# A graph layer on one core: one group of column copies moved from GpSimd's gathers to VectorE, one unchecked load a block, gates kept in PSUM, and a one-element maximum in place of a copy

## The chip, the core and the metric

The kernel runs on one core of a Trainium2 chip (trn2). The core has TensorE (PE in the profile; PEld are its weight loads), VectorE (DVE), ScalarE (ACT), GpSimd (POOL) and SyncE (SP), each with an instruction stream of its own, and DMA engines that SyncE and GpSimd feed here. The metric is the device time of one execution in microseconds; "time" is the median of several executions.

## What is computed

One layer of message passing over 12,500 nodes with 128 features and 400,000 edges, sorted by target (`dst`), each with 32 attributes. Cut to what matters:

```
h   = maximum(layernorm(x), 0)
m   = relu(concat[h[src], h[dst], ea] @ w1 + b1) @ w2 + b2
agg = segment_sum(m, dst)
gi, gh = agg @ w_ih + b_ih, h @ w_hh + b_hh
r = sigmoid(i_r + h_r); z = sigmoid(i_z + h_z); n = tanh(i_n + r * h_n)
out = x + (1 - z) * n + z * h
```

All of it is in fp32. `h[src]` is the expensive part: a row (or column) picked by a random number for each of the 400,000 edges.

## The kernel before

**Set-up.** A head normalises all nodes, keeps h transposed in SBUF (`hT_all`, 128 features x 12,500 nodes), and writes two tables to memory: A = h @ w1's first 128 rows, and B = h @ its second 128 rows + b1. It also works out, from `dst`, the first node of every group and block; SyncE, TensorE and VectorE later load such numbers into registers.

**The loop.** The edges are 3125 tiles of 128, and the tiles are 391 groups of 8 (the first has 5). One pass of the loop (`for u in range(NU)`, 782 units) does half a group. For a group, TensorE forms in PSUM the part that comes from the targets and the attributes (line 763: a one-hot matrix and the attributes in one product). The part that comes from the sources joins it in one of four ways:

- GpSimd gathers rows of A by indirect DMAs (line 193), one for each tile, eight for a group, into one of 11 buffers `G`; VectorE adds them and takes the ReLU (line 792).
- ScalarE copies columns of `hT_all`, 4 bytes in each partition, one instruction for each edge (line 1103), into a tile `HE_act`. The column's place comes from a register; 16 registers are loaded at a time (line 1090). TensorE then multiplies the tile by w1 (line 774) and VectorE takes the ReLU (line 786).
- VectorE does the same for two edges at once (class `Pairs`): one instruction (line 1061) reads two columns as bytes and writes 16-bit numbers, first + 256 x second, into `both`. For every 256 edges (`PIECE`), `part` (line 1073) parts the two bytes of each number again and writes them to `HE_dve`: 1024 bytes in each partition. A group has 512 such pairs and 4 such partings.
- SyncE fetches single rows of A by DMA.

`SPREAD` says how many groups each of VectorE, ScalarE and SyncE takes (31, 29, 5); the loop at the top spreads them evenly over the 391 groups. GpSimd has the other 326.

**Order.** Every engine's instructions stand in the order that the Python code emits them. `run_jobs` emits ScalarE's and SyncE's share of columns and rows four times a unit, evenly. VectorE's pairs are put between its other work, by due times (`some`, `behind_long`). Gathers are not issued as soon as their buffer is free: `let_go`, called four times a unit, lets one gather after another go, each behind a named instruction, twice behind VectorE's latest (`recent`) and twice behind a copy of ScalarE's (`copied`, `mark`).

**Blocks.** The sums of 14 groups make a block of 512 nodes (29 blocks; the last three are smaller). `node(b)` does a block's update as a list of steps; each `yield n` puts n units of the loop before the next step, so the steps run among the next groups' work. In order: TensorE adds up sums and degrees (tiles "nd" and "misc", one PSUM bank each); VectorE adds what the block before left over (`carry`, lines 853 and 856); TensorE makes the reset gate in "nd"; three units later ScalarE takes its sigmoid (line 902); VectorE multiplies by "misc" (line 906), adds "nd" (line 910); ScalarE takes the tanh (line 914) and the update gate's sigmoid (line 916); VectorE does the last three operations (lines 920, 923, 926); TensorE transposes, VectorE adds x (line 933), and SyncE stores. `last_node` does the last block with steps of its own. The block's first node is read by SyncE (line 830), TensorE and VectorE (line 918), and the step from the block before by VectorE (`step_of`, line 861), each with a load whose result is checked against bounds on the chip.

Of the kernel before, what the change touches and what calls it, by code (L numbers as in the profile page):

```python
# [54 lines left out]
STEP = {"act": 4, "sp": 4}  # L55
QUEUE = 10
ROW = 4 * D
SPREAD = {"dve": 31, "act": 29, "sp": 5}
START = {"dve": 14, "act": -6, "sp": 28}
SPARE = ("HE_act", "HE_dve", "G_sp")  # L60
NR = 12672
# [6 lines left out]
def tile_gnn(ctx: ExitStack, tc: tile.TileContext, x, src, srcT, dstT, dstP, eaT, eaP, w1, b1, w2T, b2,  # L68
             wih, bih, whh, bhh, out):
    nc = tc.nc  # L70
    ctx.enter_context(tc.manual_schedule())
    const = ctx.enter_context(tc.tile_pool(name="const", bufs=1))
# [108 lines left out]
    waiting, recent, copied, credit = [], [None], [None], [0]  # L181
# [140 lines left out]

    base_f = const.tile([1, NP], F32, name="base_f")
    blk_f = const.tile([1, NB], F32, name="blk_f")
    blk_i = const.tile([1, NB], I32, name="blk_i")
    off_f = const.tile([1, NB, 16], F32, name="off_f")
    off_i = const.tile([1, NB, 16], I32, name="off_i")
    base_i = const.tile([1, NB, 16], I32, name="base_i")
    step_f = const.tile([1, NB], F32, name="step_f")
    step_i = const.tile([1, NB], I32, name="step_i")  # L330
    step_c = const.tile([1, NB], F32, name="step_c")
    dloc = const.tile([128, T], F16, name="dloc")
    lim = const.tile([128, 2, NPL], F32, name="lim")
# [26 lines left out]
    def setup(pool):  # L360
        nc.vector.tensor_copy(base_f[:, 1:], base_d)
        nc.vector.memset(base_f[:, 0:1], 0.0)
        nc.vector.tensor_scalar(base_f, base_f, float(LAST), 0.0, op0=ALU.min, op1=ALU.max)
        yield
        nc.vector.tensor_copy(at_f[64:65, 512:512 + NP], base_f)
        nc.vector.tensor_tensor(at_f[64:65, :NP], at_f[64:65, 512:512 + NP], at_f[64:65, :NP], op=ALU.is_gt)
        nc.vector.tensor_reduce(beyond, at_f[64:65, :NP], AX.X, ALU.max)
        yield
        pm = ps1.tile([128, 512], F32, name="misc")
        nc.tensor.matmul(pm[:, :NP], ones, base_f, start=True, stop=True)  # L370
        nc.vector.tensor_copy(base_b[:, :, 0], pm[:, :NP])
# [10 lines left out]
        nc.vector.tensor_copy(blk_i, blk_f)  # L382
# [20 lines left out]
        nc.vector.tensor_copy(step_i, step_c)  # L403
        nc.vector.tensor_tensor(step_f, step_f, step_c, op=ALU.not_equal)
        yield
        yield
        place(0)
# [3 lines left out]
    with tc.tile_pool(name="pp", bufs=3) as pp:  # L411
# [85 lines left out]
        for q in range(NC + 3):  # L497
            if q < NC:
                b, i0, c, e, P, n0 = chunk(q)
# [3 lines left out]
            if 1 <= q <= NC:  # L503
                b, i0, c, e, P, n0 = chunk(q - 1)
# [320 lines left out]
        worked[0] = 1  # L825


    def block_start(b):
        k0, n, w = BLOCKS[b]
        g0 = nc.sync.value_load(blk_i[0:1, b:b + 1], min_val=0, max_val=N - w)  # L830
# [19 lines left out]
    def carry(b, o, p, d):  # L850
        w, last = BLOCKS[b][2], BLOCKS[max(b - 1, 0)][2]
        m = last - LEAST[b]
        nc.vector.tensor_tensor(o[:, 0:m], p[:, 0:m], o[:, bass.ds(d, m)] if b else
                                o[:, BW:BW + m], op=ALU.add)
        if m < w:
            nc.vector.tensor_copy(o[:, m:w], p[:, m:w])
        if w < last:
            nc.vector.memset(o[:, w:last], 0.0)

    def step_of(b):  # L860
        return nc.vector.value_load(step_i[0:1, b:b + 1], min_val=LEAST[b],
                                    max_val=BLOCKS[max(b - 1, 0)][2])

    def temp(w):
        return p3.tile([128, BW], F32, name="gt", bufs=3)[:, :w]

    def node(b):
        w = BLOCKS[b][2]
# [7 lines left out]
        zero(pd)  # L876
        for i in range(len(offs)):
            degree_of(b, pd, offs, i)
        d = step_of(b)
        yield 1  # L880
        carry(b, TOT, pt, d)
        carry(b, DEG[0:1, :], pd[0:1, :], d)
        worked[0] = 2
        yield 1
        g = nc.tensor.value_load(blk_i[0:1, b:b + 1], min_val=0, max_val=N - w)
# [16 lines left out]
        nc.scalar.activation(r, pr, AF.Sigmoid)  # L902
        ph = gate("misc", 3, True, False)
        yield 1
        t = temp(w)
        nc.vector.tensor_tensor(t, r, ph, op=ALU.mult)  # L906
        pi = gate("nd", 2, False, True)
        worked[0] = 2
        yield 1
        nc.vector.tensor_tensor(t, t, pi, op=ALU.add)  # L910
        pz = gate("misc", 1, True, True)
        worked[0] = 2
        yield 2 if b < NW else 1
        nc.scalar.activation(t, t, AF.Tanh)  # L914
        z = temp(w)
        nc.scalar.activation(z, pz, AF.Sigmoid)
        yield 1
        gv = nc.vector.value_load(blk_i[0:1, b:b + 1], min_val=0, max_val=N - w)
        q = r
        nc.vector.tensor_tensor(q, hT_all[:, bass.ds(gv, w)], t, op=ALU.subtract)  # L920
        worked[0] = 2
# [19 lines left out]
    def last_node():  # L941
# [5 lines left out]
        zero(pd)  # L947
        for i in range(n):
            degree_of(b, pd, offs, i)
        d = step_of(b)  # L950
        g = nc.tensor.value_load(blk_i[0:1, b:b + 1], min_val=0, max_val=N - w)
        hT = hT_all[:, bass.ds(g, w)]
        gv = nc.vector.value_load(blk_i[0:1, b:b + 1], min_val=0, max_val=N - w)
        h = hT_all[:, bass.ds(gv, w)]
        pt = ps1.tile([128, 512], F32, name="nd")[:, :w]
        zero(pt)
# [76 lines left out]
    class Pairs:  # L1033
# [35 lines left out]
        def part(self):  # L1069
            if self.turn:  # L1070
                k, p0, both = self.turn
                self.turn = None
                recent[0] = nc.vector.tensor_copy(  # L1073
                    hand[k].bitcast(U8)[:, p0 * 4:(p0 + PIECE) * 4].rearrange(
                        "p (n c b) -> p n c b", c=2, b=4),
                    both.bitcast(U8).rearrange("p n (b c) -> p n c b", c=2)).ins

    def one_by_one(m, k):
        et = {"act": ET.Activation, "sp": ET.SP}[m]
# [377 lines left out]
```

## Time and profile before

| what | value |
|---|---|
| time, median of 3 | 4675.16 us (4668.68 to 4681.94) |
| profiled execution, its time | 4666.41 us |
| profiled execution, its span | 4664.6 us |
| TensorE's granted clock, mean | 0.716 |
| DMA | 333.37 MB, mean 71 GB/s |
| gathers by GpSimd | 2605 |
| column copies by ScalarE | 29,696 |
| pairs by VectorE, partings | 15,872, 124 |

The span runs from the first to the last instruction of the program; the time holds what lies around it as well. In the rows of a profile, "idle before" is time in which an engine did nothing ahead of an instruction, with what ended it; "issue" means that nothing the profile shows ended it. ScalarE's copies overlap each other: one is shown as 189 ns long, and the next starts before it has ended, so counts per microsecond say more than durations do. Register loads are not counted as busy.

### The profile page before, as it was taken

What the parts mean: (1) busy time and instruction counts of PE and PEld (TensorE: products, weight loads), DVE (VectorE), ACT (ScalarE), POOL (GpSimd) and SP (SyncE); (2) the same over time, 40 slices, a digit from 0 to 9 for tenths busy, and PEclk for the clock granted to TensorE, in tenths of its full rate; (3) what the DMA queues carried; (4) which work ended last, traced back from release to release, by engine and by line L of the source; (5) the groups of instructions that cost most, each with busy time, mean ns of one, the idle gap of its engine ahead of it and who ended that gap; (6) DMA issues with size and microseconds to landing.
All of it is one profiled execution on the core that took longest, in us unless ns stands there. A gap on an engine that the chain in (4) does not pass through costs nothing. (4 is left out here: it accounts for less than half of the span.)

```text
span 4664.6 us, 96852 instructions
## 1 busy us (share of the span) xinstructions
PE 2538.9 (54%) x13193; PEld 1611.8 (35%) x13193; DVE 2548.3 (55%) x18124; ACT 3272.2 (70%) x29939; POOL 2485.7 (53%) x2614
## 2 busy tenths in 40 slices
PE   2465565565456455555555565455545454655657
PEld 2353342332234233323333333333323233323434
DVE  3475564564456446645654565456546555655655
ACT  2478667767767767777777767777776777676676
POOL 5345555555555555555555555555555555555551
PEclk7786767776667767776776667677767767767767
DMA  3322323222222223232222223232322322222221
GB/s 103 105 65 60 75 71 74 69 71 70 69 72 73 71 71 73 66 78 69 72 70 68 73 71 79 60 73 69 74 69 72 81 63 72 68 73 69 72 73 35
DMA packets 195490, 333.37 MB, mean 71 GB/s; under 512 B 68809, under 2 KB 117512, under 8 KB 194841
## 3 DMA queue, kind: packets, MB, share of 16 engines
q0 software_dynamic: 83360, 170.89, 16.0%
q1 hardware_dynamic: 111337, 156.20, 12.2%
q14 instruction: 539, 4.42, 0.3%
q8 instruction: 110, 1.80, 0.2%
q10 hardware_dynamic: 144, 0.07, 0.0%
HBM read 306.65 MB, written 20.24 MB: 70 GB/s over the span
## 5 line engine op out<-in xcount | busy, mean ns | idle before, releaser
L1103 ACT COPY HE_act<-hT_all 128x4 uint8 x29696 | 3169.2, 189 | 1255.9 <-issue 1223.5
L193 POOL DMA_INDIRECT G<-A,src_i x2512 | 2396.4, 954 | 2052.2 <-ACT HE_act L1103 1329.8
L1061 DVE SCALAR_TENSOR_TENSOR both<-hT_all 128x4 uint16 x15872 | 1365.4, 154 | 649.4 <-issue 635.6
L763 PE MATMUL pre<-RW,L 128*128 128x256 f32 x3128 | 1163.5, 499 | 536.3 <-DVE L L650 295.9
L763 PEld LDWEIGHTS pre<-RW,L 128*128 128x128 f32 x3128 | 681.9, 243 | 842.2 <-issue 433.3
L814 PE MATMUL seg<-RB,OH 128*32 128x129 f32 x6250 | 607.9, 325 | 270.2 <-DVE RB L792 158.4
L814 PEld LDWEIGHTS seg<-RB,OH 128*32 128x32 f32 x6250 | 334.4, 125 | 573.1 <-issue 308.9
L892 PE MATMUL nd<-DEG,brow 34*128 34x512 f32 (+2 forms) x112 | 89.0, 886 | 761.3 <-ACT gt L902 614.2
L792 DVE CUSTOM_DVE_ANT_0 RB<-pre,G 128x1024 f32<-128x1024 f32 x315 | 383.2, 1217 | 117.5 <-issue 62.9
L906 DVE TENSOR_TENSOR gt<-gt,misc 128x512 f32<-128x512 f32 (+2 forms) x28 | 18.9, 675 | 677.8 <-ACT gt L902 545.9
L892 PEld LDWEIGHTS nd<-DEG,brow 34*128 34x128 f32 x112 | 22.4, 248 | 775.7 <-ACT gt L902 620.8
L650 DVE TENSOR_TENSOR L<-L,seg 64x1024 f32<-64x1024 int32 x191 | 230.5, 1207 | 40.4 <-issue 16.4
L774 PE MATMUL pre<-w1a,HE_act 128*128 128x128 f32 x464 | 96.0, 328 | 255.0 <-ACT HE_act L1103 230.7
L786 DVE TENSOR_SCALAR RB<-pre 128x1024 f32<-128x1024 f32 x69 | 84.2, 1221 | 213.1 <-PE pre L774 154.4
L774 PEld LDWEIGHTS pre<-w1a,HE_act 128*128 128x128 f32 x464 | 90.0, 235 | 271.2 <-ACT HE_act L1103 235.6
L703 DVE TENSOR_TENSOR OH<-dloc,seg 128x512 f32<-128x512 f16 (+1 forms) x198 | 132.9, 672 | 17.6 <-issue 17.6
L842 PE MATMUL nd<-spot,sums 128*128 128x40 f32 x782 | 139.0, 358 | 2.8 <-DVE sums L823 2.8
L842 PEld LDWEIGHTS nd<-spot,sums 128*128 128x128 f32 x782 | 134.6, 270 | 13.7 <-issue 10.6
L1073 DVE COPY HE_dve<-both 128x1024 uint8<-128x1024 uint8 x124 | 88.6, 715 | 24.8 <-issue 15.7
L774 PEld LDWEIGHTS pre<-w1a,HE_dve 128*128 128x128 f32 x496 | 90.3, 226 | 14.1 <-remote 2.0
L920 DVE TENSOR_TENSOR gt<-hT_all,gt 128x512 f32<-128x512 f32 (+2 forms) x28 | 19.1, 680 | 134.3 <-ACT gt L914 109.3
L774 PE MATMUL pre<-w1a,HE_dve 128*128 128x128 f32 x496 | 89.3, 309 | 3.0 <-remote 1.7
(185 smaller groups left out, 1473.5 us busy)
## 6 DMA issues: line engine op xcount, KB each, us to landing
G_sp<-A SPq DMA_DIRECT2D x5120, 0.5 KB
L<-in_dstP SPq DMA_DIRECT2D x195, 256.0 KB
L<-in_eaP SPq DMA_DIRECT2D x195, 256.0 KB
G<-A,src_i POOLq DMA_INDIRECT x2512
RW<-B SPq DMA_DIRECT2D x782, 16.0 KB
xb<-in_x SPq DMA_DIRECT2D x26, 256.0 KB
out<-xb SPq DMA_DIRECT2D x26, 256.0 KB
xs<-in_x SPq DMA_DIRECT2D x11, 512.0 KB
```

The lines of the kernel that those rows point to most:

```text
L193: fetched = nc.gpsimd.indirect_dma_start(out=G[k][:, j, a, :], out_offset=None, in_=x if k < RAW else A, in_offset=bass.IndirectOffsetOnAx ...
L650: recent[0] = nc.vector.tensor_tensor(o.rearrange("v (k e) -> v k e", k=m), i.rearrange("v (k e) -> v k e", k=m), SEGB[(k // 2) % 2][:2 * ...
L703: recent[0] = nc.vector.tensor_tensor(p, dloc[:, e0:e1, None].to_broadcast(shape), row[:, None, :].to_broadcast(shape), op=ALU.is_equal).ins
L763: nc.tensor.matmul(p[:, 2 * i:2 * i + 2, :], Ls[k // QP][:, c0:c0 + 128], RW[k % 4], start=True, stop=not raw)
L774: nc.tensor.matmul(p[:, 2 * i + a, :], cols, w1a, start=False, stop=n + 1 == len(l) or l[n + 1][1] != j)
L792: made = nc.vector._custom_dve(TENSOR_ADD_SAT, out=o, in0=p, in1=G[k].rearrange("p j a f -> p (j a) f")[:, c, :], s0=float("inf"), s1=0.0)
L814: nc.tensor.matmul(p[r0:r0 + V, :D + 1], OH[k][:, a * GRP + j, :], RB[k % 2][:, 2 * j + a, :D + 1], start=False, stop=all(b != a for _, _, ...
L842: nc.tensor.matmul(p[:, bass.ds(offs[i], V + SHIFT)], sums[:, slot(b, i), :D], spot[:, i % 2, :], start=False, stop=i == len(offs) - 1)
L892: nc.tensor.matmul(pg, brow[:, c], DEG[:, :w], start=True, stop=False)
L1061: recent[0] = nc.vector.scalar_tensor_tensor(self.both[:, e % PIECE // 2, :], column(second), 256.0, column(first), op0=ALU.mult, op1=ALU. ...
L1073: recent[0] = nc.vector.tensor_copy(hand[k].bitcast(U8)[:, p0 * 4:(p0 + PIECE) * 4].rearrange("p (n c b) -> p n c b", c=2, b=4), both.bitc ...
L1103: copied[0] = nc.scalar.copy(he[:, e * 4:e * 4 + 4], column(v)).ins
```

## The change

Five things are altered:

- VectorE takes 32 groups of columns in place of 31; GpSimd keeps 325. VectorE's first group is then number 20 and not 21, and the places of some of VectorE's and ScalarE's groups move by one or a few.
- The parting of pairs (`part`) is a reduction by maximum over an added axis of length one. It gives the same bytes as the copy.
- The tiles `blk_i` and `step_i` go. Their numbers stand in two free columns of `off_i`, and VectorE loads both with one load a block, without a check on the chip; SyncE's and TensorE's loads of the first node have no check either.
- The carries of the sums and of the degrees lie a unit apart (in the last three blocks they follow at once, as before).
- In `node`, the candidate gate's sum is written back to its PSUM tile, where tanh is taken in place, and the update gate's sigmoid is taken in place in PSUM as well; the product r x h goes to r's own tile.

```
--- before.py
+++ after.py
@@ -55,7 +55,7 @@
 STEP = {"act": 4, "sp": 4}
 QUEUE = 10
 ROW = 4 * D
-SPREAD = {"dve": 31, "act": 29, "sp": 5}
+SPREAD = {"dve": 32, "act": 29, "sp": 5}
 START = {"dve": 14, "act": -6, "sp": 28}
 SPARE = ("HE_act", "HE_dve", "G_sp")
 NR = 12672
@@ -322,12 +322,10 @@
 
     base_f = const.tile([1, NP], F32, name="base_f")
     blk_f = const.tile([1, NB], F32, name="blk_f")
-    blk_i = const.tile([1, NB], I32, name="blk_i")
     off_f = const.tile([1, NB, 16], F32, name="off_f")
     off_i = const.tile([1, NB, 16], I32, name="off_i")
     base_i = const.tile([1, NB, 16], I32, name="base_i")
     step_f = const.tile([1, NB], F32, name="step_f")
-    step_i = const.tile([1, NB], I32, name="step_i")
     step_c = const.tile([1, NB], F32, name="step_c")
     dloc = const.tile([128, T], F16, name="dloc")
     lim = const.tile([128, 2, NPL], F32, name="lim")
@@ -379,7 +377,6 @@
             nc.vector.tensor_scalar(blk_f[:, b0:b1_], base_f[:, k0:k0 + (b1_ - b0 - 1) * n + 1:n], float(N - w),
                                     None, op0=ALU.min)
         yield
-        nc.vector.tensor_copy(blk_i, blk_f)
         nc.vector.memset(off_f, 0.0)
         off_c = pool.tile([128, NB * 16], F32, name="off_c", bufs=1)[:1, :].rearrange("o (b n) -> o b n", n=16)
         yield
@@ -400,7 +397,8 @@
         nc.vector.tensor_copy(off_i, off_c)
         yield
         nc.vector.tensor_tensor(off_f, off_f, off_c, op=ALU.not_equal)
-        nc.vector.tensor_copy(step_i, step_c)
+        nc.vector.tensor_copy(off_i[:, :, 14], step_c)
+        nc.vector.tensor_copy(off_i[:, :, 15], blk_f)
         nc.vector.tensor_tensor(step_f, step_f, step_c, op=ALU.not_equal)
         yield
         yield
@@ -825,9 +823,15 @@
         worked[0] = 1
 
 
+    def first_of(engine, b):
+        _, (g,) = nc.values_load_multi_w_load_instructions(
+            off_i[0:1, b, 15:16], engines=[engine], min_val=0, max_val=N - BLOCKS[b][2],
+            skip_runtime_bounds_check_because="clamped above")
+        return g
+
     def block_start(b):
         k0, n, w = BLOCKS[b]
-        g0 = nc.sync.value_load(blk_i[0:1, b:b + 1], min_val=0, max_val=N - w)
+        g0 = first_of(ET.SP, b)
         xb = p3.tile([128, 4, D], F32, name="xb", bufs=2)[:w // 4, :, :]
         put(xb, x[bass.ds(g0, w), :].rearrange("(p i) f -> p i f", i=4))
         _, offs = nc.values_load_multi_w_load_instructions(
@@ -858,8 +862,11 @@
             nc.vector.memset(o[:, w:last], 0.0)
 
     def step_of(b):
-        return nc.vector.value_load(step_i[0:1, b:b + 1], min_val=LEAST[b],
-                                    max_val=BLOCKS[max(b - 1, 0)][2])
+        _, (d, g) = nc.values_load_multi_w_load_instructions(
+            off_i[0:1, b, 14:16], engines=[ET.DVE], min_val=0, max_val=N - BLOCKS[b][2],
+            skip_runtime_bounds_check_because="clamped above")
+        return nc.s_assert_within(d, LEAST[b], BLOCKS[max(b - 1, 0)][2],
+                                  skip_runtime_bounds_check_because="clamped above"), g
 
     def temp(w):
         return p3.tile([128, BW], F32, name="gt", bufs=3)[:, :w]
@@ -876,13 +883,16 @@
         zero(pd)
         for i in range(len(offs)):
             degree_of(b, pd, offs, i)
-        d = step_of(b)
+        d, gv = step_of(b)
         yield 1
         carry(b, TOT, pt, d)
+        worked[0] = 2
+        if b < NW:
+            yield 1
         carry(b, DEG[0:1, :], pd[0:1, :], d)
         worked[0] = 2
         yield 1
-        g = nc.tensor.value_load(blk_i[0:1, b:b + 1], min_val=0, max_val=N - w)
+        g = first_of(ET.PE, b)
         hT = hT_all[:, bass.ds(g, w)]
 
         def gate(name, i, with_h, with_s):
@@ -902,20 +912,18 @@
         nc.scalar.activation(r, pr, AF.Sigmoid)
         ph = gate("misc", 3, True, False)
         yield 1
-        t = temp(w)
-        nc.vector.tensor_tensor(t, r, ph, op=ALU.mult)
-        pi = gate("nd", 2, False, True)
+        nc.vector.tensor_tensor(r, r, ph, op=ALU.mult)
+        t = gate("nd", 2, False, True)
         worked[0] = 2
         yield 1
-        nc.vector.tensor_tensor(t, t, pi, op=ALU.add)
+        nc.vector.tensor_tensor(t, r, t, op=ALU.add)
         pz = gate("misc", 1, True, True)
         worked[0] = 2
         yield 2 if b < NW else 1
         nc.scalar.activation(t, t, AF.Tanh)
-        z = temp(w)
-        nc.scalar.activation(z, pz, AF.Sigmoid)
+        z = pz
+        nc.scalar.activation(z, z, AF.Sigmoid)
         yield 1
-        gv = nc.vector.value_load(blk_i[0:1, b:b + 1], min_val=0, max_val=N - w)
         q = r
         nc.vector.tensor_tensor(q, hT_all[:, bass.ds(gv, w)], t, op=ALU.subtract)
         worked[0] = 2
@@ -947,10 +955,9 @@
         zero(pd)
         for i in range(n):
             degree_of(b, pd, offs, i)
-        d = step_of(b)
-        g = nc.tensor.value_load(blk_i[0:1, b:b + 1], min_val=0, max_val=N - w)
+        d, gv = step_of(b)
+        g = first_of(ET.PE, b)
         hT = hT_all[:, bass.ds(g, w)]
-        gv = nc.vector.value_load(blk_i[0:1, b:b + 1], min_val=0, max_val=N - w)
         h = hT_all[:, bass.ds(gv, w)]
         pt = ps1.tile([128, 512], F32, name="nd")[:, :w]
         zero(pt)
@@ -1070,10 +1077,10 @@
             if self.turn:
                 k, p0, both = self.turn
                 self.turn = None
-                recent[0] = nc.vector.tensor_copy(
+                recent[0] = nc.vector.tensor_reduce(
                     hand[k].bitcast(U8)[:, p0 * 4:(p0 + PIECE) * 4].rearrange(
                         "p (n c b) -> p n c b", c=2, b=4),
-                    both.bitcast(U8).rearrange("p n (b c) -> p n c b", c=2)).ins
+                    both.bitcast(U8).rearrange("p n (b c) -> p n c b", c=2)[:, :, :, :, None], AX.X, ALU.max).ins
 
     def one_by_one(m, k):
         et = {"act": ET.Activation, "sp": ET.SP}[m]
```

More of the change, by code (lines that the diff above doesn't have):

```diff
@@ L57 @@
 ROW = 4 * D
-SPREAD = {"dve": 31, "act": 29, "sp": 5}
+SPREAD = {"dve": 32, "act": 29, "sp": 5}
 START = {"dve": 14, "act": -6, "sp": 28}
@@ L324, in tile_gnn @@
     blk_f = const.tile([1, NB], F32, name="blk_f")
-    blk_i = const.tile([1, NB], I32, name="blk_i")
     off_f = const.tile([1, NB, 16], F32, name="off_f")
@@ L329, in tile_gnn @@
     step_f = const.tile([1, NB], F32, name="step_f")
-    step_i = const.tile([1, NB], I32, name="step_i")
     step_c = const.tile([1, NB], F32, name="step_c")
@@ L381, in setup @@
         yield
-        nc.vector.tensor_copy(blk_i, blk_f)
         nc.vector.memset(off_f, 0.0)
@@ L402, in setup @@
         nc.vector.tensor_tensor(off_f, off_f, off_c, op=ALU.not_equal)
-        nc.vector.tensor_copy(step_i, step_c)
+        nc.vector.tensor_copy(off_i[:, :, 14], step_c)
+        nc.vector.tensor_copy(off_i[:, :, 15], blk_f)
         nc.vector.tensor_tensor(step_f, step_f, step_c, op=ALU.not_equal)
@@ L825, in take, with first_of @@
         worked[0] = 1
+    def first_of(engine, b):
+        _, (g,) = nc.values_load_multi_w_load_instructions(
+            off_i[0:1, b, 15:16], engines=[engine], min_val=0, max_val=N - BLOCKS[b][2],
+            skip_runtime_bounds_check_because="clamped above")
+        return g
     def block_start(b):
         k0, n, w = BLOCKS[b]
-        g0 = nc.sync.value_load(blk_i[0:1, b:b + 1], min_val=0, max_val=N - w)
+        g0 = first_of(ET.SP, b)
         xb = p3.tile([128, 4, D], F32, name="xb", bufs=2)[:w // 4, :, :]
@@ L860, in step_of @@
     def step_of(b):
-        return nc.vector.value_load(step_i[0:1, b:b + 1], min_val=LEAST[b],
-                                    max_val=BLOCKS[max(b - 1, 0)][2])
+        _, (d, g) = nc.values_load_multi_w_load_instructions(
+            off_i[0:1, b, 14:16], engines=[ET.DVE], min_val=0, max_val=N - BLOCKS[b][2],
+            skip_runtime_bounds_check_because="clamped above")
+        return nc.s_assert_within(d, LEAST[b], BLOCKS[max(b - 1, 0)][2],
+                                  skip_runtime_bounds_check_because="clamped above"), g
     def temp(w):
@@ L878, in node @@
             degree_of(b, pd, offs, i)
-        d = step_of(b)
+        d, gv = step_of(b)
         yield 1
         carry(b, TOT, pt, d)
+        worked[0] = 2
+        if b < NW:
+            yield 1
         carry(b, DEG[0:1, :], pd[0:1, :], d)
@@ L884, in node @@
         yield 1
-        g = nc.tensor.value_load(blk_i[0:1, b:b + 1], min_val=0, max_val=N - w)
+        g = first_of(ET.PE, b)
         hT = hT_all[:, bass.ds(g, w)]
@@ L904, in node @@
         yield 1
-        t = temp(w)
-        nc.vector.tensor_tensor(t, r, ph, op=ALU.mult)
-        pi = gate("nd", 2, False, True)
+        nc.vector.tensor_tensor(r, r, ph, op=ALU.mult)
+        t = gate("nd", 2, False, True)
         worked[0] = 2
         yield 1
-        nc.vector.tensor_tensor(t, t, pi, op=ALU.add)
+        nc.vector.tensor_tensor(t, r, t, op=ALU.add)
         pz = gate("misc", 1, True, True)
@@ L914, in node @@
         nc.scalar.activation(t, t, AF.Tanh)
-        z = temp(w)
-        nc.scalar.activation(z, pz, AF.Sigmoid)
+        z = pz
+        nc.scalar.activation(z, z, AF.Sigmoid)
         yield 1
-        gv = nc.vector.value_load(blk_i[0:1, b:b + 1], min_val=0, max_val=N - w)
         q = r
@@ L949, in last_node @@
             degree_of(b, pd, offs, i)
-        d = step_of(b)
-        g = nc.tensor.value_load(blk_i[0:1, b:b + 1], min_val=0, max_val=N - w)
+        d, gv = step_of(b)
+        g = first_of(ET.PE, b)
         hT = hT_all[:, bass.ds(g, w)]
-        gv = nc.vector.value_load(blk_i[0:1, b:b + 1], min_val=0, max_val=N - w)
         h = hT_all[:, bass.ds(gv, w)]
@@ L1072, in part @@
                 self.turn = None
-                recent[0] = nc.vector.tensor_copy(
+                recent[0] = nc.vector.tensor_reduce(
                     hand[k].bitcast(U8)[:, p0 * 4:(p0 + PIECE) * 4].rearrange(
                         "p (n c b) -> p n c b", c=2, b=4),
-                    both.bitcast(U8).rearrange("p n (b c) -> p n c b", c=2)).ins
+                    both.bitcast(U8).rearrange("p n (b c) -> p n c b", c=2)[:, :, :, :, None], AX.X, ALU.max).ins
     def one_by_one(m, k):
```

## The prediction

> **What bounds the kernel now.** I read the page first, then the waits of each engine, then stretches of the loop side by side. The page:
>
> ```profile
> span 4664.6 us, 96852 instructions
> ...
> PE 2538.9 (54%) x13193; PEld 1611.8 (35%) x13193; DVE 2548.3 (55%) x18124; ACT 3272.2 (70%) x29939; POOL 2485.7 (53%) x2614
> ```
>
> No engine looks full; ScalarE (ACT) is the busiest. The waits of ScalarE (engine, line, released by: us in total, times, longest) say what its other 30% is:
>
> ```profile
> ACT HE_act L1103 <- issue: 1223.5, 2104, 1.9
> ...
> ACT gt L991 <- PE pre L972: 22.1, 1, 22.1
> ...
> ACT HE_act L1103 <- ACT HE_act L1103: 0.7, 3, 0.3
> ```
>
> In the whole loop ScalarE waits for nobody. Its 1223.5 us of pauses between column copies are "issue": nothing that the profile shows holds it. The one real wait, 22.1 us, comes after the last copy. The copies fill the run:
>
> ```profile
> L1103 ACT COPY HE_act<-hT_all x29696: 176/189/198, 168.1 to 4632.6; 128x4 uint8 x200
> ```
>
> They start at 168.1 us and end at 4632.6; 32.0 us later the program is over. So time = 168.1 + the chain of 29,696 copies + 32.0. VectorE, by contrast, stands and waits, mostly for ScalarE (the rows of line 786 through TensorE's products of ScalarE's columns):
>
> ```profile
> DVE gt L906 <- ACT gt L902: 545.9, 22, 36.2
> DVE RB L786 <- PE pre L774: 154.4, 19, 25.6
> DVE gt L920 <- ACT gt L914: 109.3, 22, 7.2
> DVE gt L906 <- ACT HE_act L1103: 86.6, 4, 31.3
> ...
> DVE gt L906 <- remote: 45.3, 2, 30.3
> ```
>
> Together 941.5 us of slack on VectorE. GpSimd has slack too; in the groups (busy, mean ns | idle before, released by):
>
> ```profile
> L193 POOL DMA_INDIRECT G<-A,src_i x2512 | 2396.4, 954 | 2052.2 <-ACT HE_act L1103 1329.8 <-issue 538.8 <-DMA dst_i<-in_dstT 77.2
> L1061 DVE SCALAR_TENSOR_TENSOR both<-hT_all 128x4 uint16 x15872 | 1365.4, 154 | 649.4 <-issue 635.6
> ```
>
> The gathers are released behind ScalarE's copies and wait 1329.8 us for them. Why then does ScalarE pause? Two timelines of the same 10 us, GpSimd's and ScalarE's:
>
> ```profile
> 2011.74 0.94 POOL L193 DMA_INDIRECT G<-A,src_i  x1 [3.92 <-ACT HE_act L1103]
> ...
> 2016.73 0.95 POOL L193 DMA_INDIRECT G<-A,src_i  x1 [0.30 <-issue]
> ```
> ```profile
> 2009.09 6.10 ACT L1103 COPY HE_act<-hT_all 128x4 uint8 x60 [1.13 <-issue]
> 2016.02 0.38 ACT L1103 COPY HE_act<-hT_all 128x4 uint8 x3 [0.84 <-issue]
> 2017.45 0.38 ACT L1103 COPY HE_act<-hT_all 128x4 uint8 x3 [1.04 <-issue]
> ```
>
> Five gathers start back to back from 2011.74; from the third or fourth on, ScalarE falls from 60 copies in 6.1 us to 3 in about 1.4. It pauses when gathers come in a row. Stretches of the loop (us; then busy time and instructions of PE, PEld, DVE, ACT, POOL; granted clock, DMA share, GB/s) give the price:
>
> ```profile
> 170.00:4590.00 4420.00, 2409.57 (x12506) 1509.47 (x12507) 2429.85 (x17551) 3164.43 (x29359) 2416.20 (x2533) 0.71 0.29 71
> 4590.00:4632.00 42.00, 34.78 (x203) 23.19 (x204) 25.33 (x139) 41.01 (x409) 0.00 (x0) 0.85 0.14 40
> 2011.00:2043.00 32.00, 1.69 (x14) 1.17 (x12) 0.00 (x0) 25.52 (x246) 18.86 (x20) 0.55 0.32 76
> 2070.00:2102.00 32.00, 20.57 (x109) 12.64 (x109) 23.23 (x160) 21.26 (x197) 16.56 (x18) 0.77 0.28 74
> 1846.00:1882.00 36.00, 0.00 (x0) 0.00 (x0) 0.38 (x4) 29.33 (x278) 22.47 (x24) 0.50 0.28 67
> 1884.00:1920.00 36.00, 25.74 (x131) 15.57 (x130) 24.62 (x169) 27.43 (x252) 21.02 (x22) 0.79 0.31 74
> ```
>
> ScalarE does 6.64 instructions per us in the loop (29,359 in 4420), 9.7 once the gathers are over (409 in 42). Beside VectorE and TensorE at rest it does 7.7 (246 in 32; 278 in 36), beside both at work 6.2 and 7.0: on the mean 1.1 per us less.
>
> **The change, part by part.** ScalarE keeps its 29 groups, so only what alters the pace of its copies counts.
>
> *One group from GpSimd to VectorE.* Eight gathers go (2605 to 2597), 512 pairs come. If ScalarE's pauses belong to the gathers evenly, one costs 1223.5/2605 = 0.47 us, eight 3.8. The bounds: zero, and the whole loop per gather, 4420/2533 = 1.745 us, eight 14.0. I take -3.8, since pauses are what a gather was seen to cause. A group on VectorE costs (1365.4 + 649.4)/31 = 65 us with its register loads; that lies in the 941.5 us of slack. But VectorE at work slows ScalarE: 65 us at 1.1 per us are 72 copies, at 6.64 per us 10.8 us. In the rows compared TensorE works too, and its work does not grow: of the 378 instructions of PE, PEld and DVE in the stretch from 2070, 160 are VectorE's, 42%: 4.6 us. I take +4.6, with 0 and 10.8 as bounds.
>
> *The maximum for the copy.* No one-element maximum is in the trace. The copy:
>
> ```profile
> L1073 DVE COPY HE_dve<-both 128x1024 uint8<-128x1024 uint8 x124 | 88.6, 715 | 24.8 <-issue 15.7 <-DVE both L1061 7.2 <-remote 1.8
> ```
>
> The nearest rows are another operation over 1024 elements, and a reduction of 160 elements to one:
>
> ```profile
> L792 DVE CUSTOM_DVE_ANT_0 RB<-pre,G 128x1024 f32<-128x1024 f32 x315 | 383.2, 1217 | 117.5 <-issue 62.9 <-PE pre L763 24.2 <-DVE both L1061 22.2
> ```
> ```profile
> L357 DVE TENSOR_REDUCE lim<-dloc 128x1 f32<-128x160 f16 (+2 forms) x20 | 6.3, 316 | 0.7
> ```
>
> The copy's 715 ns for 1024 elements is far under line 792's 1217; the reduction, with 316 ns for 160, shows no such speed. At the pace of line 792 the maximum takes 1.22 us; 128 of them 156.2, against 88.6: 67.6 us more on VectorE. If a result for every element costs an element's time again, it is about 2.3 us, 294 in all, 206 more; if it kept the copy's pace, only the four more, 3 us. Nearest is line 792, for its 1024 results: 1.22. All this lies in the slack; on ScalarE's chain 0, since it adds four instructions. If being busy alone disturbed ScalarE, 67.6 us at the price above would be 11.2. The Trainium skill speaks against this edit (VectorE: DVE Perf Modes, section on the perf-mode tier table): a copy has a two-element mode, the reduction none, 1227 against 2293 ns for 2048 fp32 elements. By that ratio a part takes 1.34 us as an estimate, 83 us more in all; the slack covers this as well, so the sum stays.
>
> *One unchecked load a block.* A checked load on VectorE:
>
> ```profile
> L861 DVEq TENSOR_LOAD <-step_i x29: 304/307/619, 387.6 to 4638.2; - x29
> L861 DVEq FUSED_REGOPS  x29: 183/190/210, 388.0 to 4638.9; - x29
> L861 DVEq SEQ_ASSERT  x29: 23/23/41, 388.3 to 4639.1; - x29
> ```
>
> 0.52 us; two in each of 29 blocks, 30 us, become 29 loads without the two other steps, 9 us: -21 us on VectorE, the same steps gone from TensorE and SyncE, none on ScalarE: 0. VectorE's sum is 65 + 67.6 - 21 = +112 us, and 830 us of slack remain. Were this cover gone, the 112 us would all be on the path.
>
> *Carries apart.* The degree's carry comes one unit later and so does everything behind it in a block; a block's steps take 20 of 28 units in place of 19, so the next block isn't touched, and ScalarE meets its sigmoid one unit later among copies that it does anyway: 0.
>
> *Gates in PSUM.* Tanh and the second sigmoid write PSUM, and tanh reads it:
>
> ```profile
> L914 ACT ACTIVATE gt<-gt 128x512 f32<-128x512 f32 (+2 forms) x28 | 17.2, 615 | 0.0
> ...
> L916 ACT ACTIVATE gt<-misc 128x512 f32<-128x512 f32 (+2 forms) x28 | 15.8, 565 | 0.6 <-issue 0.6
> ```
>
> A PSUM source is 50 ns cheaper: -1.4 us for 28 tanhs. A PSUM result is not in the trace; I take no difference, 1.4 either way. The banks "nd" and "misc" are held up to the products on VectorE, but their next users come behind those products already: no new wait.
>
> Sum on ScalarE's chain: -3.8 + 4.6 - 1.4 = -0.6 us, nothing. Against the profiled execution's 4666.4 us that is 4666; the median of the runs shown, 4675.2, lies 8.8 higher, so I put the forecast at 4675. About 0.3%, 14 us, is what a measurement can tell from no change.
>
> **The rivals.** *Slower: ScalarE is disturbed by VectorE's time, not by its instructions.* All 112 us at 1.1 copies per us cost 123 copies, 18.6 us, and with the least relief from gathers (0) and none from PSUM, 4694. It decides from 0.83 copies per us on (14 us). For it: both pairs of stretches. Against it: TensorE is in both.
>
> *Slower by far: VectorE becomes the bound.* That needs a maximum of (941.5 - 65 + 21 + 88.6)/128 = 7.7 us; at 10 us the time would be near 4970. No row points to that.
>
> *Faster: the copy's hold on GpSimd goes.* Against a floor of 944 ns for a gather, the 2512 of line 193 take 25 us too long in sum (954 - 944 = 10 ns each); if the copies cause that, and the rows of gathers then start later and end later over ScalarE, up to 25 us come back: 4650. With the other bound of the eight gathers alone (-14.0) 4661. The Trainium skill (SBUF — State Buffer, section on who interferes with whom) has this rule: a copy in a two-port mode takes the port pair shared with GpSimd for the whole instruction, a reduction on trn2 never does. Against a gain: GpSimd waits 1329.8 us for ScalarE, so its own delays are not on the path.
>
> **How the numbers follow.** No change within 14 us: 0.48. Faster by the hold or the gathers: 0.26. Slower by VectorE's time: 0.23, by a very dear maximum 0.03. The range reaches to the rivals: down to 4645, which is 4650 without the 4.6 us that the forecast charges for the pairs; up to 4702, the slower rival at its worse pair of stretches (7.69 - 6.16 = 1.53 copies per us, 25.8 us) without the 1.4 of PSUM. The likeliest case's own range is 4661 to 4689.
>
> **What would show it.** Right: ScalarE's copies 29,696 with issue pauses of 1200 to 1250 us and no wait on others in the loop; the waits of lines 906, 920 and 786 on VectorE shorter by some 110 us; 128 maxima near 1.2 us; 16,384 pairs; 2597 gathers. Wrong: ScalarE waiting for VectorE or TensorE at a gate, pauses outside 1200 to 1250, or a maximum above 7 us.

## The result and the profile after

The changed kernel takes 4697.22 us against 4678.12 (medians of 6 runs each): ratio 1.0042, interval 1.0032 to 1.0052. It is slower by 19 us, more than the 14 us inside which "no change" was forecast. The profiled execution took 4693.54 us against 4666.41, 27 us more; the one of before lies 12 us under its median and the one after 4, so about 8 of the 27 are chance.

The experiments below were spread over five chips. On three of them the kernel before takes 4607 to 4677 us, on the other two 3321 and 3323; every ratio is to the kernel before on the same chip. One of the 23 executions of the kernel before on the second chip took 7719 us and is left out of its ratios.

The page after, as it was quoted of before:

```profile
span 4691.4 us, 97156 instructions
...
PE 2571.0 (55%) x13209; PEld 1630.1 (35%) x13209; DVE 2656.7 (57%) x18640; ACT 3276.2 (70%) x29939; POOL 2459.8 (52%) x2606
```

VectorE is busy 108 us longer, ScalarE as long as before. ScalarE's copies (instructions: shortest, middle, longest ns, first and last start in us) and the waits of its copies and of its last gate, from two views:

```profile
L1110 ACT COPY HE_act<-hT_all x29696: 176/189/207, 168.0 to 4659.7; 128x4 uint8 x200
```
```profile
ACT HE_act L1110 <- issue: 1244.4, 2138, 2.6
...
ACT gt L998 <- PE pre L979: 21.2, 1, 21.2
```

The frame of the prediction stands: head 168.0 us, tail 31.7, and the chain of copies between them, which sets the time. All that was lost was lost inside the chain, 27.2 us, and no new wait shows there: its pauses without a visible cause grew from 1223.5 to 1244.4. VectorE's waits for ScalarE, and the groups that the change touches:

```profile
DVE gt L915 <- ACT gt L912: 508.9, 23, 36.0
DVE RB L784 <- PE pre L772: 101.6, 18, 24.9
DVE gt L928 <- ACT nd L923: 93.4, 18, 7.7
...
DVE gt L915 <- ACT HE_act L1110: 60.6, 3, 25.8
...
DVE gt L915 <- remote: 20.9, 1, 20.9
```
```profile
L193 POOL DMA_INDIRECT G<-A,src_i x2504 | 2370.4, 947 | 2097.7 <-ACT HE_act L1110 1409.1
L1068 DVE SCALAR_TENSOR_TENSOR both<-hT_all 128x4 uint16 x16384 | 1406.5, 154 | 644.0 <-issue 629.5
...
L1080 DVE TENSOR_REDUCE HE_dve<-both 128x1024 uint8<-128x1024 uint8 x128 | 155.3, 1213 | 29.7 <-issue 19.7
```
```profile
L923 ACT ACTIVATE nd<-nd 128x512 f32<-128x512 f32 (+2 forms) x28 | 15.8, 566 | 0.6 <-issue 0.6
```

VectorE still waits 785.4 us in these five rows (the five of before gave 941.5, and some 110 less was forecast): it isn't the bound here. A maximum takes 1213 ns (1.22 us was forecast), the tanh in PSUM 566 (565 was forecast), and the mean gather has become 7 ns shorter.

The whole loop and its end without gathers, in the views that gave ScalarE's pace before (time, then busy us and instructions of PE, PEld, DVE, ACT, POOL):

```profile
170.00:4590.00 4420.00, 2424.21 (x12443) 1517.63 (x12443) 2518.86 (x17932) 3140.89 (x29092) 2390.27 (x2525) 0.70 0.29 70
4617.00:4659.00 42.00, 34.90 (x205) 23.35 (x205) 24.29 (x128) 41.53 (x413) 0.00 (x0) 0.84 0.11 33
```

ScalarE does 6.58 instructions per us beside the gathers in place of 6.64, and still 9.8 without them.

### The profile page after: what moved, and what is told of

Same layout as the page of the kernel before. It is cut to its first block, busy times and chain, and to the rows that moved or that the text cites. A ratio compares the mean times of both kernels' runs of the same rounds, so it can differ in the third digit from the quotient of the medians.

```text
span 4691.4 us, 97156 instructions
## 1 busy us (share of the span) xinstructions
PE 2571.0 (55%) x13209; PEld 1630.1 (35%) x13209; DVE 2656.7 (57%) x18640; ACT 3276.2 (70%) x29939; POOL 2459.8 (52%) x2606
## 5 line engine op out<-in xcount | busy, mean ns | idle before, releaser
L1110 ACT COPY HE_act<-hT_all 128x4 uint8 x29696 | 3173.5, 189 | 1278.4 <-issue 1244.4
L193 POOL DMA_INDIRECT G<-A,src_i x2504 | 2370.4, 947 | 2097.7 <-ACT HE_act L1110 1409.1
L1068 DVE SCALAR_TENSOR_TENSOR both<-hT_all 128x4 uint16 x16384 | 1406.5, 154 | 644.0 <-issue 629.5
L812 PE MATMUL seg<-RB,OH 128*32 128x129 f32 x6250 | 624.1, 332 | 404.1 <-DVE RB L790 241.1
L1080 DVE TENSOR_REDUCE HE_dve<-both 128x1024 uint8<-128x1024 uint8 x128 | 155.3, 1213 | 29.7 <-issue 19.7
L906 PE MATMUL nd<-TOT,w2ih 128*128 128x512 f32 (+2 forms) x112 | 91.8, 915 | 0.0
```

Of the source, the lines that this page charges most:

```text
L193: fetched = nc.gpsimd.indirect_dma_start(out=G[k][:, j, a, :], out_offset=None, in_=x if k < RAW else A, in_offset=bass.IndirectOffsetOnAx ...
L812: nc.tensor.matmul(p[r0:r0 + V, :D + 1], OH[k][:, a * GRP + j, :], RB[k % 2][:, 2 * j + a, :D + 1], start=False, stop=all(b != a for _, _, ...
L1068: recent[0] = nc.vector.scalar_tensor_tensor(self.both[:, e % PIECE // 2, :], column(second), 256.0, column(first), op0=ALU.mult, op1=ALU. ...
L1080: recent[0] = nc.vector.tensor_reduce(hand[k].bitcast(U8)[:, p0 * 4:(p0 + PIECE) * 4].rearrange("p (n c b) -> p n c b", c=2, b=4), both.bi ...
L1110: copied[0] = nc.scalar.copy(he[:, e * 4:e * 4 + 4], column(v)).ins
```

## The experiments

Each run is named by its number, e1 to e18. Theories: **A**, VectorE's 512 more pairs slow ScalarE's copies beside them. **B**, the copy's hold on GpSimd's ports kept gathers from following each other; without it rows get longer and ScalarE pauses more. **C**, VectorE's busy time in general disturbs ScalarE (the slower rival of the prediction). **D**, the edits in the blocks cost.

**One part taken back, one part alone.** Four kernels on one chip (the kernel before: 4606.8 us).

The changed kernel with the copy back (e1):

```
-                recent[0] = nc.vector.tensor_reduce(
+                recent[0] = nc.vector.tensor_copy(
...
```

> The changed kernel with the copy back in place of the maximum; all else as changed. The changed kernel stands 19 us (0.42%) over the one before. Theory A (the 512 more pairs and their loads slow ScalarE's copies beside them, as instructions): still +15 to +20 us. Theory B (the copy's hold on the port pair parted rows of gathers; without it the rows are longer and ScalarE pauses more): 0 to +5 us. Theory C (VectorE's longer busy time disturbs ScalarE, whatever it does): 0 to +7 us, by the 67 us that the copy saves of 112. Theory D (the edits in the blocks): still +19 us. Under A and D rows of five or more gathers stay as frequent as in the changed kernel (253 of 672 rows), under B they fall back to some 230 of 721.

Measured: 1.0047 (1.0033 to 1.0060). Rows of five or more gathers, counted as starts at most 1.4 us apart, are 264 of 721 in its trace, 256 of 746 in that of before and 276 of 707 after the change; they decide nothing.

The changed kernel with `"dve": 31` (e2):

> The changed kernel with 31 groups on VectorE in place of 32, the maximum and the block edits kept. A: 0 to +5 us over the kernel before. B: still +15 to +20. C: +8 to +12 (VectorE busy some 47 us more than before). D: +19.

Measured: 1.0022 (1.0009 to 1.0034).

The kernel before with the maximum alone (e3, the opposite of the first diff):

> The kernel before with the maximum in place of the copy, nothing else. A: 0. B: +15 to +20 us and longer rows of gathers. C: +11 (67 of 112 us of VectorE's time). D: 0.

Measured: 1.0013 (0.9998 to 1.0027).

The kernel before with `"dve": 32` alone (e4):

> The kernel before with 32 groups on VectorE in place of 31, nothing else. A: +15 to +20 us. B: 0 to +3. C: +8 to +11 (65 us of VectorE's time). D: 0.

Measured: 1.0015 (1.0003 to 1.0028).

B falls: with the copy back the kernel is as slow as ever. C is in trouble for the same reason, since the copy saves VectorE some 65 us. Neither A nor D explains the whole: 32 groups alone cost 7 us where A wanted 15 to 20, and the other edits with 31 groups (e2) 10 us where D wanted 19.

**The blocks alone, and the prices made large.** Four kernels on a second chip (before: 4608.43 us). The block edits alone, with 31 groups and the copy (e5):

> The kernel before with the block edits alone (one unchecked load a block, carries apart, gates in PSUM); 31 groups, the copy. The first four runs left, by sums, 0.1 to 0.3% for these edits (with the copy back the changed kernel stood at 1.0047, 32 groups alone at 1.0015; 31 groups at 1.0022, the maximum alone at 1.0013). Theory D (the block edits cost most of it): 1.002 to 1.003. Theory A (VectorE's pairs) with no cost in the blocks: 1.000.

Measured: 1.0009 (0.9997 to 1.0021), +4 us.

Half of the pairs left out (e6). Each instruction that stays writes its sum to two places, so that the columns of every second pair are missing:

```
-                recent[0] = nc.vector.scalar_tensor_tensor(
-                    self.both[:, e % PIECE // 2, :], column(second), 256.0, column(first),
...
+                if self.done % 2 == 0:
+                    at2 = e % PIECE // 2
+                    recent[0] = nc.vector.scalar_tensor_tensor(
+                        self.both[:, at2:at2 + 2, :], column(second)[:, None, :].to_broadcast([128, 2, 4]), 256.0,
...
```

> The kernel before with every second pair instruction left out: one instruction writes the same sum to two places, so half of the columns on VectorE are wrong, and 7936 instructions fewer run there; register loads, copies, gathers and their order stay. Theory A (ScalarE's pace beside VectorE's instructions: 7 us for 512 pairs and their loads, so some 14 ns a pair): 4607 less 100 to 130 us. If VectorE's instructions are off ScalarE's chain altogether: 0 to -10 us.

Measured: 4559.29 us (two runs), 0.9894 (0.9869 to 0.9919), -49 us. That is 6.2 ns for each of the 7936 pairs left out, so 3.2 us for 512 of them, less than half of what A needs, and less than the 4.6 us of the prediction. Taken as a price of VectorE's time it can be had from the pages of e5 and e6, on the same chip:

```profile
PE 2565.2 (55%) x13193; PEld 1623.8 (35%) x13193; DVE 2544.1 (55%) x18124; ACT 3272.2 (71%) x29939; POOL 2482.4 (54%) x2614
```
```profile
PE 2498.1 (55%) x13193; PEld 1592.1 (35%) x13193; DVE 1971.8 (43%) x10188; ACT 3264.7 (72%) x29939; POOL 2495.3 (55%) x2614
```

VectorE is busy 572 us less, so the price is 0.09 us for each of them, half of what C takes (1.1 copies per us at 6.64 copies per us, 0.17). At half its price C gives some 10 of the 19 us.

28 groups on ScalarE, 32 on VectorE (e7):

```
-SPREAD = {"dve": 31, "act": 29, "sp": 5}
+SPREAD = {"dve": 32, "act": 28, "sp": 5}
```

> The kernel before with 28 groups on ScalarE and 32 on VectorE: one group moves from ScalarE to VectorE, gathers stay. If the copies' chain bounds (time = head + copies + tail), with pauses that belong to the gathers: 1024 copies at 0.105 us go, -108 us, +7 for the pairs: -100 us. If pauses scale with the copies: -154 + 7 = -147. If something shared by all engines bounds, and not ScalarE's own chain: within 15 us of the kernel before.

Measured: 4554.39 us (two runs), 0.9883 (0.9858 to 0.9908), -54 us: less than any reckoning by the copies' own time, more than nothing. Its chain of copies and its pauses, and after them those of the next kernel (e8), which keeps 29 groups on ScalarE, and has 36 on VectorE and 40 gathers fewer:

```profile
L1103 ACT COPY HE_act<-hT_all x28672: 176/189/197, 168.8 to 4520.9; 128x4 uint8 x200
```
```profile
ACT HE_act L1103 <- issue: 1207.7, 2133, 1.9
```
```profile
L1103 ACT COPY HE_act<-hT_all x29696: 176/189/197, 169.0 to 4575.0; 128x4 uint8 x200
```
```profile
ACT HE_act L1103 <- issue: 1156.2, 2095, 1.9
```

With 1024 copies fewer the pauses are not fewer but 51 us more (and 21 us more than the 1186.7 of e5, which has as many gathers as e7): they don't scale with the copies. A copy costs 151.8 ns there (4352.1 us by 28,672) and 148.4 here. So ScalarE's chain is what ends last, but only half of the 108 us of which it was to be relieved is gained; the single traces put 21 to 51 us of the rest down to pauses.

36 groups on VectorE, 321 on GpSimd (e8):

> The kernel before with 36 groups on VectorE and 321 on GpSimd: five groups moved where the change moves one. If the cost is one of the pairs and linear: five times the 7 us of 32 groups, +35 us (1.0076). If 32 groups cost by their places among the other groups and not by their number: within 10 us of the kernel before. If fewer gathers relieve ScalarE by 0.47 us each with nothing against it: -19 us.

Measured: 1.0011 (0.9998 to 1.0023), +5 us for five groups, 1 us each. This speaks against C: five groups are 325 us of VectorE's time, which at C's price would cost 54 us less the relief from 40 gathers, 19 us at the prediction's 0.47 us for a gather. No run measured that relief by itself; at the prediction's upper bound of 1.745 us for a gather (70 us) it would hide C. The 1 us is also what the prediction's two terms gave for a group (-3.8 + 4.6 = +0.8). The 7 us of e4 (1 to 13) can't then be the price of a group: they are chance in part, or belong to the places of the groups.

**Which block edit, beside 32 groups.** Four kernels on a third chip (before: 4677.35 us). The changed kernel again (e9):

> The changed kernel itself, beside the three below on one chip: 1.004 to 1.005 of the kernel before, as on record (1.0042). If the single edits only add up (32 groups 0.15%, the maximum 0.13%, the blocks 0.09%): 1.0037. With the copy back it stood at 1.0047, so by that pair the maximum costs nothing, by the single edit 0.13%.

Measured: 1.0048 (1.0035 to 1.0060).

The three others have 32 groups and the copy, and one block edit each is taken back. Both carries in one step (e10):

```
         carry(b, TOT, pt, d)
-        worked[0] = 2
-        if b < NW:
-            yield 1
         carry(b, DEG[0:1, :], pd[0:1, :], d)
```

> 32 groups, the copy, unchecked loads, gates in PSUM, but both carries in one step as before. If the later carry (every step of a block a unit later) is what makes 32 groups dear with the block edits (1.0047 with all of them, 1.0015 without any): 1.0015 to 1.002. If not: 1.004 to 1.005.

Measured: 1.0013 (1.0000 to 1.0025).

The gates' tiles in SBUF (e11):

```
-        nc.vector.tensor_tensor(r, r, ph, op=ALU.mult)
-        t = gate("nd", 2, False, True)
+        t = temp(w)
+        nc.vector.tensor_tensor(t, r, ph, op=ALU.mult)
+        pi = gate("nd", 2, False, True)
...
-        z = pz
-        nc.scalar.activation(z, z, AF.Sigmoid)
+        z = temp(w)
+        nc.scalar.activation(z, pz, AF.Sigmoid)
```

> 32 groups, the copy, unchecked loads, carries apart, but the gates' tiles in SBUF as before. If holding the PSUM banks longer, or ScalarE's writes to PSUM, cost: 1.0015 to 1.002. If not: 1.004 to 1.005.

Measured: 1.0005 (0.9994 to 1.0016).

The loads checked, from `blk_i` and `step_i`, as before (e12):

> 32 groups, the copy, carries apart, gates in PSUM, but the checked loads as before. Loads off ScalarE's chain: 1.004 to 1.005. If the unchecked loads let VectorE, TensorE and SyncE run on where their sequencers stood, and that disturbs ScalarE: 1.0015 to 1.003. If the three block edits are noise and 32 groups stand at 1.0015 whatever is beside them, all three kernels lie at 1.001 to 1.003.

Measured: 1.0035 (1.0023 to 1.0048). So with 32 groups the later carry and the gates in PSUM seem to cost some 0.3% together, and either of them without the other next to nothing (theory **E**); the loads are off it. Against E stands e5, where both together, beside 31 groups, cost 0.09%. The alternative (theory **F**): the steps' and groups' places happen to fall well or badly.

**Four kernels on a chip without the pauses** (before: 3321.05 us). They were meant to part E from F and to try ScalarE's pauses. The changed kernel with the carries together (e13), and with 33 groups (e14):

> The changed kernel with both carries in one step, all else as changed. Theory E (the later carry together with the gates in PSUM costs 0.2 to 0.35%; either alone does not): 1.001 to 1.002. If the later carry matters only beside the copy: 1.004 to 1.005.

Measured: 1.0181 (1.0167 to 1.0195), +61 us.

> The changed kernel with 33 groups on VectorE in place of 32. If the cost is that of the block edits whenever VectorE has more work (E): 1.004 to 1.006. Theory F (it hangs on how the groups' places fall beside the blocks' steps, so that one more group can take it away): 1.000 to 1.003, as with 31 groups (1.0022).

Measured: 1.0371 (1.0356 to 1.0385), +124 us. A small write of GpSimd's behind every gather in the kernel before (e15):

```
             fetched = nc.gpsimd.indirect_dma_start(
...
+            nc.gpsimd.memset(idle_t, 0.0)
```

> The kernel before with a small write of GpSimd's (a tile of zeros that nothing reads) behind every gather, about 0.2 to 0.25 us, so that gathers in a row start some 1.5 us apart and not 1.25. If ScalarE pauses because gathers follow too close: fewer than 24% of the loop with four gathers in the last 5 us, and 40 to 150 us less. If it pauses for the number of gathers, not their distance: within 15 us of the kernel before, or slower, since rows take longer.

Measured: 1.0920 (1.0903 to 1.0936). 26 groups on ScalarE and 34 on VectorE (e16):

> The kernel before with 26 groups on ScalarE and 34 on VectorE (three groups moved from ScalarE to VectorE). One group gave -54 us (28 on ScalarE): three give -160, 0.966, if ScalarE's chain still bounds; with VectorE's waits for ScalarE then used up, it and not ScalarE is late, and the gain is smaller, -60 to -120.

Measured: 1.0696 (1.0680 to 1.0712).

None answers its question, since the pauses are missing there. Slowing the gathers costs there (in e15 VectorE waits 355.6 us for landings), and so does work moved to VectorE: three groups from ScalarE 231 us (e16), and the 33rd group, between e13 and e14, 62 us, where the prediction reckons 65 us for a group's work.

```profile
DVE RB L794 <- DMA G<-A,src_i: 355.6, 102, 10.0
```

**The changed kernel (e17) and its carries together (e18), once more** (a fifth chip, again without pauses, before: 3323.15 us):

> The changed kernel, beside the one with the carries together. On a chip where ScalarE pauses beside the gathers (the kernel before at 4600 to 4700 us): 1.004 to 1.005, as twice. On a chip where it does not (the kernel before at 3321 us): VectorE has no slack there, so the 112 us of its sum count; with the carries together it stood at 1.0181 (+61 us), so 1.015 to 1.035.

Measured: 1.0179 (1.0165 to 1.0193), +57 us.

> The changed kernel with both carries in one step. On a chip with pauses, theory E (the later carry with the gates in PSUM costs 0.2 to 0.35%): 1.001 to 1.002; theory F (accident of places): anything from 1.000 to 1.005. On a chip without: 1.0181 as before, and the changed kernel equal to it within 10 us if the later carry is off the path there.

Measured: 1.0184 (1.0170 to 1.0198). The later carry is nothing there. The changed kernel's page on this chip, ScalarE's copies and waits, and what is left of VectorE's idle time, most of it ahead of its own pairs:

```profile
PE 2435.7 (72%) x13209; PEld 1573.3 (47%) x13209; DVE 2619.7 (78%) x18640; ACT 3098.1 (92%) x29939; POOL 2464.5 (73%) x2606
```
```profile
L1110 ACT COPY HE_act<-hT_all x29696: 177/189/207, 93.9 to 3340.1; 128x4 uint8 x200
```
```profile
ACT nd L923 <- DVE nd L919: 83.2, 19, 8.4
ACT gt L912 <- PE nd L906: 58.9, 10, 16.1
ACT HE_act L1110 <- issue: 31.2, 78, 1.1
```
```profile
DVE both L1068 <- issue: 465.2, 790, 1.8
DVE RB L790 <- issue: 37.7, 75, 1.3
DVE RB L790 <- DVE both L1068: 30.8, 54, 0.8
DVE L L648 <- issue: 25.4, 46, 1.2
DVE RB L790 <- PE pre L761: 19.6, 29, 3.6
```

Here the picture is turned round: ScalarE's pauses are 31.2 us in place of 1244.4, and it waits 83.2 and 58.9 us at the gates for VectorE and TensorE, while no wait for ScalarE is among VectorE's long ones. VectorE's cover is gone. For that case the prediction put all of its 112 us on the path; the kernel lost 57. The kernel before has no trace on such a chip, so which of these waits are new isn't shown.

## Why the prediction was wrong

*What held.* ScalarE's chain sets the time (head and tail moved by less than half a microsecond; a group taken off ScalarE gives 54 us). A group moved from GpSimd to VectorE has a price of about 1 us (e8), as the two terms together had it. That is in part luck: a pair costs 6.2 ns (e6), so the second term was 3.2 and not 4.6, and the first was never measured by itself. The maximum takes 1213 ns, tanh and the second gate are as cheap as reckoned, no gate made ScalarE wait. The rule that the reduction leaves GpSimd's ports alone (the Trainium skill, SBUF — State Buffer, section on who interferes with whom) agrees with the mean gather's 947 ns after 954: in the traces of all chips with pauses it is 953 to 958 ns beside copies and 946 to 950 beside maxima. As the argument against that rival said, it bought nothing: GpSimd waits 1409.1 us for ScalarE. By the ratio of the other page (the Trainium skill, VectorE: DVE Perf Modes, section on the perf-mode tier table) the maximum was to take 1.34 us, an estimate; 1213 ns decides for the row of line 792.

*What failed.* The sum on ScalarE's chain, -0.6 us, by its noughts: "on ScalarE's chain 0" for the maximum, 0 for the carries apart, "no new wait" for the gates in PSUM, and by the step of pricing each edit alone and adding up. Each of the three parts alone measured a little above its term: 32 groups +7 us (1.4 to 13) for +0.8, the maximum +6 (-1 to 12) for 0, the blocks +4 (-1.4 to 10) for -1.4. Their sum, 0.37%, lies within the interval of the whole (0.32 to 0.52%). But the kernel with the copy back speaks against a plain sum: without the maximum 0.24% is left to expect, and e1 measured 0.47% (0.33 to 0.60), as much as the whole. By that the maximum's nought held, and as far as these runs tell it is the noughts of the carries and gates that failed, beside 32 groups: with the copy in all three, the loss is 0.35% where both edits are there (e12, its loads checked), 0.13% without the later carry (e10), 0.05% without the gates in PSUM (e11). Beside 31 groups the same two edits cost 0.09% (e5).

*By what.* By ScalarE's pauses for the most part: of the 27.2 us by which the traced chain is longer, 20.9 are pauses and 4.3 the copies' own busy time. These are single executions, and they vary by as much: the traced one of e5 took 23 us more than the median of its kernel. The traces of the third chip agree, with pauses of 1243 and 1244 us in e9 and e12, 1232 and 1235 in e10 and e11. The prediction had the price of pauses from two pairs of stretches, where VectorE and TensorE stood or worked, and spread it over VectorE's instructions. The slower rival took the same price for VectorE's time and came to 4694, close to the 4697 measured. That is luck as far as the runs show: by it the copy put back should have returned 11 us (returned: none), and five groups cost 54 less the relief from the gathers (cost: 5). At the half price of e6 the rival isn't excluded, but it then explains half of the loss at most.

One reading of the prediction holds on some chips only: that pauses are what a gather causes. In the trace after the change ScalarE loses 0.39 us in each us to pauses where three or more gathers have started within the last 5 us, and 0.04 where fewer have. On two chips the gathers follow each other for long stretches, and ScalarE hardly pauses. What the chips differ in isn't shown. The marks set for right or wrong were also too weak: "pauses of 1200 to 1250 us" was met at 1244.4.

*What stays open.* Which edit the loss belongs to. In e1 and e9 to e12 it seems to need 32 groups, the later carry and the gates in PSUM together; that would be an effect of how the steps fall in time. For the whole change the single edits with their intervals allow a plain sum as well; for e1 they are 0.23% short, where the three intervals together allow some 0.22%. Why ScalarE should pause more for these edits no run shows. Repeats of the changed kernel with the carries together on a chip with pauses would part the two; both runs of it fell on chips without. That the pauses depend on the distance between gathers was tried only where there are none.

*A better kernel.* None is shown to be faster on all chips. 28 groups on ScalarE and 32 on VectorE gained 1.17% where ScalarE pauses; 26 and 34 lost 7% where it doesn't, and neither was run on the other kind of chip.

## What to carry to other kernels

An engine that stands and waits is cover only as long as the engine it waits for is slow, and here that was a matter of the chip: in the changed kernel VectorE waits 785 us in the rows shown on one chip, and next to nothing for ScalarE on another. The same edits, which make a slack engine longer, cost 19 us on the one and 57 on the other, so such an edit should be priced for both. And where an engine's idle time is "issue", released by nothing that the profile shows, a term of half a percent can't be had by sums of a few us each. Prices were to be had by making an edit large (half the pairs, five groups), and even these didn't add up to the loss: edits that go in together should be measured together.

## What the runs showed of the hardware

Unexpected was the difference between chips. Of the five chips of the experiments, three ran the kernel before in 4607 to 4677 us and two in 3321 and 3323, 28 to 29% less, with hardly any spread among their runs (3319 to 3326). In the traces of the changed kernel the copies start at 93.9 us in place of 168.0; ScalarE's pauses are 31.2 us in place of 1244.4, and the chain of 29,696 copies, with what lies between them, takes 109 ns for each (3246.2 us in all) in place of 151. On the chip without pauses gathers run at the same 1.25 us apart, for ten in a row in this stretch (of which the first and the last are shown):

```profile
1999.66 0.94 POOL L193 DMA_INDIRECT G<-A,src_i  x1 [0.30 <-issue]
...
2010.90 0.98 POOL L193 DMA_INDIRECT G<-A,src_i  x1 [0.30 <-issue]
```

In e13, on the other such chip, ScalarE makes 52 copies in 5.35 us beside four gathers in a row:

```profile
1999.83 5.35 ACT L1107 COPY HE_act<-hT_all 128x4 uint8 x52
```

The pauses aren't ScalarE's alone. SyncE makes one register move for each of the 5120 rows that it fetches. These moves in the changed kernel (shortest, middle, longest ns), on the chip with pauses and on the one without:

```profile
L110 SPq MOVE G_sp<-A x5120: 2/29/787, 371.8 to 4548.9; - x197
```
```profile
L110 SPq MOVE G_sp<-A x5120: 29/29/59, 230.3 to 3250.5; - x197
```

In the first trace 1688 of ScalarE's pauses are longer than 0.4 us. Inside them SyncE starts 0.5 instructions per us, on the mean of the run 3.0, and in 73% of them one starts within 0.06 us of the pause's end (30% would at its mean pace). So SyncE mostly stands still with ScalarE; what stops them, no run shows.

Smaller: an unchecked load of two registers on VectorE takes 535 ns, where a load of one took 307, so that the block edits saved VectorE 15 us and not 21.

```profile
L865 DVEq TENSOR_LOAD <-off_i x29: 531/535/956, 387.3 to 4664.5; - x29
```
